# Layer 1's way back on VectorE in blocks of 32, the residual added in rows by GpSimd, the importance as a row through DRAM

## The chip, the cores and the metric

The kernel runs on one core of a Trainium2 chip. A core has TensorE (PE, matrix products and transposes), VectorE (DVE), ScalarE (ACT), GpSimd (POOL) and SyncE (SP, which here only issues transfers), 16 DMA engines, and two on-chip memories: SBUF, and PSUM, which PE writes. The metric is the device time of one execution in microseconds; lower is better. Everything is fp32.

## The reference

x has 8 images of C = 512 channels and N = 1024 positions (32 x 32). Two layers follow each other.

Layer 0: group norm (32 groups), then attention with 8 heads of 64 over all 1024 positions, a projection, and the residual: `x = x + proj(attention(norm(x)))`.

Layer 1 works on the result:

```
importance = nan_to_num(sum(xf * xf, axis=1))        # per position
idx = top_k(importance, 256)
q, k, v = wq xf, wk xf, wv xf                        # v for all positions
q_sel, k_sel = layer_norm(q[idx]), layer_norm(k[idx])
attended = softmax(clip(q_sel k_sel^T * C**-0.5)) v[idx]
out = v with its columns idx replaced by attended
x = x + wo out
```

## The kernel before, in words

Layer 0 takes 64 units (8 images, 4 pairs of heads, 2 halves of the positions). A unit has 8 blocks of scores; a list written out by hand, `SLOT`, gives the order of all steps of all units, some ahead of their unit. Beside the attention, PE fills in the projections of other images. `project_out` (line 789) makes a [128, 512] piece of the layer's output in a PSUM bank; VectorE adds bias and residual (line 796), and SP stores the piece to `x1_dram` (line 799). The bank of these fillings is a single one, so the next filling waits until it has been read.

Layer 1 (lines 244 to 605) takes one image (batch) after another. `BATCH` is one period of its order, written out by hand: each word is a step; `+` and `-` say for which batch, relative to the period, the step is done. So steps of four batches are mixed in a period. `END` is the order of the last part. All five engines keep this order, and each engine runs its instructions in order. A batch's steps, with their lines:

- `load_x1` (204) loads the image from `x1_dram`, [channel, position]. Odd batches use the tiles of layer 0's q and k, even ones a tile `x1`.
- `row` (245) transposes 128 positions on PE into a PSUM bank, four transposes of 128x128. `square` (250) sums the squares on ACT, `keep` (255) copies the rows to SBUF, `put` (258) stores them to `x_dram` from ACT's queue.
- `finite` (261) cleans the importance, a column per 128 positions. `spread` (269) makes a row of it on all 128 partitions by transposing the broadcast column on PE, 8 transposes; `imp` (277) copies it to SBUF.
- `count` (281), 8 per batch on VectorE, finds for each position how many are more important: the ones before it in order with "at least", the ones after with "more than", and within its own 128 columns the ties by a triangular mask `before`. `place`, `pick`, `holder`, `who` (328 to 357) turn the counts into the positions of the 256 chosen; `holder` is a product of PE.
- `vo` (306) gives wo wv x as rows, four products per 128 positions (wo and wv are multiplied once, at the end of layer 0); `vkeep` (314) copies them to a tile V, `vput` (325) stores them to `v_dram`.
- `getx`, `getv` (359) gather the chosen rows of x and of the values by indirect DMAs on GpSimd's queue; `vsel` (372) computes the last batch's chosen values instead.
- `selt`, `selk`, `qk` (386 to 408) make q and k of the chosen; `stats`, `root`, `norm` (410 to 437) are the layer norm, its row on VectorE, its square root on ACT; `normt`, `scale` (439 to 464) turn it back and apply weight and bias, q on ACT, k on VectorE.
- `score`, `clip`, `exp`, `probt`, `probk`, `att`, `attk` (466 to 525) are the attention of the chosen, `attput` (527) stores its 256 rows, and `fetch` (533) overwrites, by 8 indirect DMAs, the chosen rows of V.
- The way back: `back` (546) transposes V to [channel, position] on PE, four transposes for a [128, 512] piece, 8 pieces a batch; `add` (555) adds the residual on VectorE, reading the PSUM bank, and SP stores the result. `residual` (541) loads that residual from `x1_dram`, for the last two batches it is the x tile itself.

Between the layers, `begin_layer1` (1135) and `finish` (1157) do batch 0's rows, importance, counts and values beside the last projections of layer 0; `finish` puts each `count` of batch 0 between two projections.

Of the kernel before, what the change touches and what calls it, by code (L numbers as in the profile page):

```python
# [9 lines left out]
F32 = mybir.dt.float32  # L10
# [8 lines left out]
P = 128  # L19
# [20 lines left out]
BLOCKS = 2 * HALF // BLOCK  # L40
ET = mybir.EngineType
# [19 lines left out]
vkeep6- square1 inv-- put4 put2 holder- add3--- keep1 square2 back4--- att0-- att1-- who-  # L61
row6 put1 row0 add4--- row7 keep0 back7--- square0 row3 keep6 attk0-- put0 square3 vo0 row5
vput7- square6 getx- vput4- attk1-- keep3 square7 square5 add7--- vput5- back6--- keep7
finite vo1 attput-- add6--- vput0- vkeep0 keep5 selt1- selt0- spread1 spread0 fetch1-- imp1 imp0
count2 fetch0-- put6 count5 vo3 count7 vkeep1 selk1- selk0- qk1- count6 count3 qk0-
fetch5-- qk2- vput6- vput3- stats0- stats1- vput2- qk3- root0- stats2- root2- fetch2-- norm0-
vkeep3 put5 norm2- vput1- root1- vo4 vkeep4 stats3- fetch3-- norm1- vo2 root3- back0--
fetch6-- fetch4-- norm3- fetch7-- normt1- normt0- count4 vkeep2 add0-- put3 put7 back5--
normt2- normt3- scale2- scale3- row4+ add5-- back1-- scale1- count0 back2-- vo5 scale0-
count1 square4+ keep4+ place score0- score1- clip- back3-- vo6 vkeep5 pick0 add1-- exp- vo7  # L70
getv- add2-- pick1 row2+ probt- vkeep7 row1+ probk- keep2+
"""
END = """
vput2-- put4- vkeep6-- row3- add3---- square2- holder-- att1--- back4---- row0- who-- inv---
put2- row7- square1- keep1- attk1--- att0--- getx-- square3- keep3- keep0- keep7- put1- put3-
put7- row5- back6---- attk0--- row6- square7- back7---- square6- add4---- square0- square5-
keep5- keep6- put0- vput5-- vo1- put5- selt1-- finite- vkeep1- spread1- add6---- add7----
selk1-- selt0-- spread0- imp1- imp0- attput--- count1- vo0- row6 row2 vput7-- selk0-- count6-
keep6 keep2 row1 square2 count0- count2- vput6-- count7- row0 count3- vkeep0- square1 keep1
put1 vput1-- qk0-- row7 qk1-- put6- square0 put2 stats1-- qk3-- stats0-- count5- put6 keep7  # L80
square6 vo7- put7 root1-- vput1- fetch5--- row4 root0-- norm0-- qk2-- keep0 stats3--
fetch3--- count4- vo6- place- square4 vkeep7- keep4 norm1-- square7 root3-- stats2-- row3
vput0- vkeep6- vo4- normt1-- root2-- norm3-- normt0-- vput0-- row5 keep3 fetch1--- vput4--
vput3-- norm2-- vkeep4- scale1-- normt2-- put3 normt3-- scale0-- fetch2--- pick1- scale2--
square5 square3 keep5 put5 vo2- fetch0--- pick0- holder- finite spread0 scale3-- put4 vkeep2-
imp0 getv-- fetch6--- spread1 who- imp1 score0-- back2--- count4 score1-- fetch7--- count2
clip-- exp-- count3 vput2- back0--- count7 getx- vput4- count6 put0 add0--- vo3- count0
fetch4--- probt-- vkeep3- probk-- inv-- add2--- att0-- att1-- attk1-- attk0-- selt1- selt0-
selk1- selk0- attput-- count5 fetch6-- count1 qk3- place stats3- pick0 back3--- back4---
vput6- add4--- root3- pick1 back1--- qk2- fetch4-- qk0- fetch0-- norm3- add3--- fetch2--  # L90
vput7- back7--- stats2- stats0- holder fetch3-- fetch1-- qk1- who vput3- add7--- root0-
root2- add1--- back5--- norm2- getx add5--- back6--- vo5- normt3- stats1- norm0- fetch7--
root1- fetch5-- norm1- normt2- vkeep5- add6--- normt0- normt1- back2-- scale0- scale3-
scale2- back5-- back7-- vput5- add2-- back1-- add1-- selt1 back6-- back3-- scale1- add7--
add5-- score0- add6-- back0-- selt0 score1- selk1 add3-- clip- selk0 qk2 exp- stats2 back4--
qk1 probt- probk- stats1 getv- add0-- qk0 qk3 att1- root2 root1 norm2 norm1 stats0 inv-
stats3 add4-- root0 attk1- vo1 att0- root3 norm3 vkeep1 norm0 attk0- normt3 normt2 normt0
attput- scale3 normt1 fetch5- scale0 scale1 fetch7- fetch6- vo0 vkeep0 scale2 score1 fetch1-
score0 clip vsel1 fetch4- vo3 exp vselk1 vsel0 vselk0 probt fetch0- probk fetch2- vkeep3 vo6
att1 inv fetch3- att0 vo7 vkeep6 vo2 back0- attk1 back2- back4- attk0 vkeep7 back3- attput  # L100
vkeep2 add3- add0- back5- vo4 fetch7 fetch3 vo5 vkeep4 add2- back1- back7- fetch2 back6-
fetch0 fetch1 add4- add1- fetch6 add7- add5- back2 back4 add4 add6- back0 back6 fetch4 vkeep5
add0 fetch5 back3 back7 add2 back1 add6 back5 add3 add7 add1 add5
# [15 lines left out]
def attention_then_topk_attention(  # L119
# [49 lines left out]

    xp = ctx.enter_context(tc.tile_pool(name="xp", bufs=1))  # L170
# [6 lines left out]
    a_dram = [dram.tile([TOP, C], F32, tag=f"sa{b}", name=f"sa{b}") for b in range(B)]  # L177


    before = const.tile([P, P], F32, tag="before", name="before")  # L180
    iota_f = const.tile([P, TOP], F32, tag="iota_f", name="iota_f")
    token = const.tile([P, NB, 2], BF16, tag="token", name="token")

    def constants():
        w["ln_w"] = vector_of(ln_w, CT, "lw")
        w["ln_b"] = vector_of(ln_b, CT, "lb")
        make_lower_triangular(nc, before, val=1.0, diag=False)
        nc.gpsimd.iota(
            iota_f, pattern=[[1, TOP]], base=0, channel_multiplier=0,
            allow_small_or_imprecise_dtypes=True,  # L190
        )

        part = const.tile([P, 2, NB], F32, tag="part", name="part")
        nc.gpsimd.iota(
            part[:, 0, :], pattern=[[0, NB]], base=0, channel_multiplier=1,
            allow_small_or_imprecise_dtypes=True,
        )
        nc.gpsimd.iota(
            part[:, 1, :], pattern=[[P, NB]], base=0, channel_multiplier=0,
            allow_small_or_imprecise_dtypes=True,  # L200
        )
        nc.vector.tensor_copy(token, part.rearrange("p k a -> p a k"))

    def load_x1(b):

        if b % 2 and b < B - 1:
            x1[b] = [qk_tile(tag, i, f"x1_{b}_{tag}{i}") for tag in "qk" for i in range(2)]
        else:
            if b == B - 1:
                t = pools["x2"].tile([P, CT, N], F32, tag="x2", name=f"x1_{b}")  # L210
            else:
                t = xp.tile([P, CT, N], F32, tag="x1", name=f"x1_{b}")
            x1[b] = [t[:, c, :] for c in range(CT)]
        for c in range(CT):
            nc.sync.dma_start(x1[b][c], x1_dram[b][:, c, :])

    def load_layer1():
# [4 lines left out]
        load_x1(0)  # L222
# [26 lines left out]

    def square(b, j):  # L250
        norm = get("r1", ("norm", b), [P, NB], "norm", 2)
        sq = keep_pool.tile([P, C], F32, tag="sq", name=f"sq_{b}_{j}", bufs=1)
        nc.scalar.activation(sq, tiles["pt", b, j], AF.Square, accum_out=norm[:, j : j + 1])

    def keep_row(b, j):
        nc.scalar.copy(get("r1", ("xT", b, j), [P, C], "xT", XT), tiles["pt", b, j])

    def put(b, j):
        nc.scalar.dma_start(x_dram[b][ts(j, P), :], tiles["xT", b, j])
# [9 lines left out]
    def spread_row(b, j):  # L269
        pi = bank(("pi", b, j))  # L270
        for i in range(NB // 2):
            nb = j * (NB // 2) + i
            nc.tensor.transpose(
                pi[:, ts(i, P)], tiles["col", b][:, nb : nb + 1].broadcast_to([P, P]), ident
            )

    def imp(b, j):
        t = get("rp", ("imp", b), [P, N], "imp", 1)
        nc.scalar.copy(t[:, ts(j, HALF)], tiles["pi", b, j])

    def count(b, j):
# [3 lines left out]
        mine = tiles["col", b][:, j : j + 1]  # L285
        lo, hi = j * P, (j + 1) * P
        junk = tiles.get("junk")
        if junk is None:
            junk = pools["rp"].tile([P, N], F32, tag="junk", name=f"junk_{b}_{j}", bufs=1)
        if lo:  # L290
            nc.vector.tensor_scalar(
                junk[:, :lo], imps[:, :lo], mine, None, ALU.is_ge, ALU.add,
                accum_out=cnt[:, 0, j : j + 1],
            )
        else:
            nc.vector.memset(cnt[:, 0, 0:1], 0.0)
        nc.vector.tensor_scalar(  # L297
            junk[:, lo:], imps[:, lo:], mine, None, ALU.is_gt, ALU.add,
            accum_out=cnt[:, 1, j : j + 1],
        )  # L300
        nc.vector.scalar_tensor_tensor(
            junk[:, lo:hi], imps[:, lo:hi], mine, before, ALU.is_equal, ALU.mult,
            accum_out=cnt[:, 2, j : j + 1],
# [10 lines left out]
    def vkeep(b, j):  # L314
        if ("V", b) not in tiles:
            if b % 3:
                tiles["V", b] = pools["up"].tile([P, NB, C], F32, tag=f"V{b % 3}", name=f"V_{b}")
            else:
# [956 lines left out]
```

## Time and profile before

| | us |
|---|---|
| median of 3 runs | 2460.2 |
| the runs | 2457.78, 2460.20, 2460.57 |
| the profiled execution | 2458.73 |
| its span, first to last instruction | 2457.0 |

The granted clock of TensorE was 0.999 of full speed. Each group of the profile gives the line, engine and operation, what is written and read, the shapes, the number of instructions, their busy time, the mean duration of one, and the idle time of the engine just before with what ended it. PE's records are shown two to a program's fp32 product. Transfers, with the median time from issue to landing:

```profile
x<-x1d SPq DMA_DIRECT2D x20, 512.0 KB, 6.7
sa<-att SPq DMA_DIRECT2D x8, 512.0 KB, 5.4
out_dram<-x SPq DMA_DIRECT2D x16, 256.0 KB, 3.4
V<-sa,at POOLq DMA_INDIRECT x64, 3.0
```

### The profile page before, as it was taken

Reading aid. Unit: us, or ns where it says so; the run is one execution under the profiler, and the core shown is the slowest. Engines: PE = TensorE matmul, PEld = TensorE weight load, DVE = VectorE, ACT = ScalarE, POOL = GpSimd, SP = SyncE. Lnnn points to the kernel's source line nnn. Section 1 sums busy time; section 2 is a strip of 40 time slices with the busy share of each in tenths; the row PEclk is TensorE's granted clock in tenths of the full one; section 3 lists DMA queues with packets and bytes.
Section 4 is the critical chain, followed back from the end, with each engine's and each line's share of the span. In section 5 each row is a group of like instructions: output and inputs, shape, how many; then the busy total and the mean of one; then the engine's idle time right before and its main releaser. Section 6 shows DMA issues by size and latency. Waiting matters only on the chain. (4 is left out here: it accounts for less than half of the span.)

```text
span 2457.0 us, 32002 instructions
## 1 busy us (share of the span) xinstructions
PE 2410.3 (98%) x11724; PEld 967.2 (39%) x11724; DVE 1949.5 (79%) x2946; ACT 1405.2 (57%) x1828; POOL 1162.9 (47%) x557
## 2 busy tenths in 40 slices
PE   7999999999999999999999999999999999999998
PEld 3333333333333333333333333333333345555554
DVE  4899988988898889888988897889777466666683
ACT  2667666665666567656766676567656524333421
POOL 0556645655555556645655555556545501111122
PEclk9999999999999999999999999999999999999999
DMA  3011112111211120112011211112112444666553
GB/s 137 25 33 65 35 54 66 55 44 48 86 40 48 51 84 31 44 61 78 27 49 60 74 39 49 61 37 67 57 57 99 145 139 155 210 209 240 192 190 107
DMA packets 108252, 205.55 MB, mean 84 GB/s; under 512 B 19114, under 2 KB 19370, under 8 KB 108096
## 3 DMA queue, kind: packets, MB, share of 16 engines
q1 hardware_dynamic: 82432, 159.95, 19.5%
q10 hardware_dynamic: 18144, 31.48, 3.4%
q0 software_dynamic: 7520, 12.09, 1.7%
q8 instruction: 92, 1.51, 0.3%
q14 instruction: 64, 0.52, 0.1%
HBM read 146.29 MB, written 69.73 MB: 88 GB/s over the span
## 5 line engine op out<-in xcount | busy, mean ns | idle before, releaser
L1014 POOL TENSOR_TENSOR es<-es,e 128x1024 f32<-128x1024 f32 x384 | 913.6, 2379 | 61.3 <-ACT e L1009 33.2
L955 ACT COPY e<-sc 128x1024 f32<-128x1024 f32 x512 | 510.2, 1009 | 379.0 <-DVE high L961 265.9
L1006 DVE TENSOR_TENSOR e<-e,ns 128x1024 f32<-128x1024 f32 x512 | 593.7, 1210 | 0.6 <-ACT ns L1002 0.3
L1009 ACT ACTIVATE e<-e 128x1024 f32<-128x1024 f32 x512 | 532.1, 1056 | 49.6 <-DVE e L1006 36.2
L1014 POOL TENSOR_TENSOR es<-e,e 128x1024 f32<-128x1024 f32 x64 | 152.5, 2383 | 817.3 <-ACT e L1009 817.3
L947 PE MATMUL sc<-q,k 64*128 64x512 f32 x2048 | 509.9, 615 | 6.8 <-ACT e L955 6.5
L961 DVE TENSOR_TENSOR high<-sc,high 128x1024 f32<-128x1024 f32 x384 | 467.4, 1217 | 46.8 <-PE sc L947 28.3
L1022 PE MATMUL av<-e,v 128*64 128x512 f32 x2048 | 476.2, 596 | 4.6 <-DVE o L1064 3.2
L744 PE MATMUL g<-x,wqkv 128*64 128x512 f32 x1984 | 453.1, 598 | 0.7 <-ACT v L783 0.7
L947 PEld LDWEIGHTS sc<-q,k 64*128 64x128 f32 x2048 | 175.4, 185 | 309.3 <-issue 213.9
L1022 PEld LDWEIGHTS av<-e,v 128*64 128x64 f32 x2048 | 144.2, 137 | 303.8 <-issue 285.4
L744 PEld LDWEIGHTS g<-x,wqkv 128*64 128x64 f32 x1984 | 131.3, 136 | 306.9 <-issue 292.1
L744 PE MATMUL g<-wqkv,x 128*64 128x256 f32 x1920 | 220.4, 382 | 0.0
L744 PE MATMUL g<-o,wp 128*64 128x512 f32 x912 | 207.0, 595 | 0.0
L1051 DVE RECIPROCAL rs<-rs 128x256 f32<-128x256 f32 x64 | 112.1, 1751 | 94.3 <-ACT rs L1045 94.3
L744 PEld LDWEIGHTS g<-wqkv,x 128*64 128x64 f32 x1920 | 132.5, 137 | 106.0 <-issue 34.7
L534 POOL DMA_INDIRECT V<-sa,at x64 | 64.3, 1005 | 154.8 <-ACT selT L396 49.7
L961 DVE TENSOR_TENSOR high<-sc,e 128x1024 f32<-128x1024 f32 x64 | 77.6, 1213 | 59.8 <-ACT e L955 59.1
L744 PEld LDWEIGHTS g<-o,wp 128*64 128x64 f32 x912 | 64.4, 137 | 134.1 <-issue 117.9
L309 PE MATMUL b_pv<-w,x 128*128 128x512 f32 x256 | 114.1, 592 | 0.0
L405 PE MATMUL b_pp<-w,selT 128*128 128x512 f32 x256 | 112.6, 594 | 0.9 <-ACT selT L396 0.7
L363 POOL DMA_INDIRECT sel<-sx,who x16 | 16.1, 1007 | 193.4 <-PE b_po L550 47.9
(177 smaller groups left out, 1988.2 us busy)
## 6 DMA issues: line engine op xcount, KB each, us to landing
nb<-negd SPq DMA_DIRECT2D x128, 256.0 KB, 3.5
x<-in_x_dram SPq DMA_DIRECT2D x32, 512.0 KB, 5.3
ri<-rsd SPq DMA_DIRECT2D x128, 128.0 KB, 2.8
sx<-xT ACTq DMA_DIRECT2D x64, 256.0 KB, 3.3
xr<-in_x_dram SPq DMA_DIRECT2D x58, 256.0 KB, 3.4
x1d<-xr SPq DMA_DIRECT2D x58, 256.0 KB, 4.0
sv<-V ACTq DMA_DIRECT2D x56, 256.0 KB, 3.1
y<-x1d SPq DMA_DIRECT2D x48, 256.0 KB, 4.5
```

Of the source, the lines that this page charges most:

```text
L309: nc.tensor.matmul(pv, x1[b][k][:, ts(j, P)], w["vo"][:, k, :], start=(k == 0), stop=(k == CT - 1),)
L405: nc.tensor.matmul(pp, tiles["selT", b][:, k, ts(rb, P)], w["qk"[which]][:, k, :], start=(k == 0), stop=(k == CT - 1),)
L534: nc.gpsimd.indirect_dma_start(tiles["V", b][:, j, :], None, a_dram[b][:, :], bass.IndirectOffsetOnAxis(ap=tiles["at", b][:, j : j + 1], a ...
L744: nc.tensor.matmul(out[r, :], wide_[:, r], moving, start=(k == 0), stop=(k == CT - 1),)
L947: nc.tensor.matmul(sc[:, hh, :], ks[p][r, ts(j, P)], qs[p][r, ts(hf, HALF)], start=True, stop=True,)
L955: nc.scalar.copy(raw[t, j], banks["s", t, j])
L961: nc.vector.tensor_tensor(high[t], banks["s", t, j], raw[t, 0] if j == 1 else high[t], ALU.max)
L1006: nc.vector.tensor_tensor(raw[t, j], raw[t, j], high[t], ALU.add)
L1009: nc.scalar.activation(raw[t, j], raw[t, j], AF.Exp, scale=QK_SCALE)
L1014: nc.gpsimd.tensor_add(sums[t], raw[t, 0] if j == 1 else sums[t], raw[t, j])
L1022: nc.tensor.matmul(avs[t][HD * hh : HD * hh + HD, :], vs[p // 2][:, j, (p % 2) * P + HD * hh : (p % 2) * P + HD * hh + HD], e[:, hh, :], s ...
L1051: nc.vector.reciprocal(rs[:, : HALF // 2], rs[:, : HALF // 2])
```

## The change

1. Positions are taken in another order. `project_out` writes each half (512 positions) of layer 0's output to `x1_dram` with columns permuted: position 4p + j goes to column 128j + p (4 = J). VectorE reads the bank and the residual with a step of four elements and writes a new tile. A tile of 128 columns so holds the positions 4p + j of a half, and its rows in DRAM lie J apart. `put` becomes two stores of half an image on SP, 8 KB per partition.
2. The rows of x stay in a tile R, which takes the place of V as the batch's store; `vkeep` now fills one of four small tiles, `vput` stores it, and `resid` adds it to R on GpSimd. `attk` adds the chosen rows of x to the attention's result. `fetch` overwrites rows of R.
3. The way back: `back` takes 256 channels of 512 positions with four block transposes of VectorE (32x32 within [128, 256]), written with a step of four elements; `store` writes the result with four transfers of 32 partitions, in runs of 128 positions. No residual is loaded and no `add` remains. For the last batch PE does the way back as before (`pback`), copied by VectorE and ACT (`ykeep`) into one of the four tiles shared with `back`, and stored (`yput`).
4. Importance: `nput` stores the column to DRAM, `nget` loads it as a row on all partitions; `spread` and `imp` go. `count` compares with the position's half instead of its 128 columns; ties are tested over 512 columns by a mask of 516.
5. `stats`, `var`, `root`, `factor` take two blocks of rows at a time; `norm` and both halves of `scale` are on ACT. `holder` has three columns.
6. `BATCH` and `END` are new orders; periods begin at -2 and x tiles are loaded in the list's order, one of four parts a step.

The diff, cut to its core:

```
 def keep_row(b, j):
-    nc.scalar.copy(get("r1", ("xT", b, j), [P, C], "xT", XT), tiles["pt", b, j])
-def put(b, j):
-    nc.scalar.dma_start(x_dram[b][ts(j, P), :], tiles["xT", b, j])
+    nc.scalar.copy(rows(b)[:, j, :], tiles["pt", b, j])
+def put(b, h):
+    nc.sync.dma_start(
+        x_dram[b][ts(h, HALF), :].rearrange("(p j) c -> p j c", j=J), rows(b)[:, ts(h, J), :])
...
-def spread_row(b, j):
-    pi = bank(("pi", b, j))
...
+def nput(b, _):
+    nc.sync.dma_start(n_dram[b].rearrange("(h p j) -> p h j", h=NH, j=J),
+        tiles["col", b].rearrange("p (h j) -> p h j", h=NH))
+def nget(b, _):
+    nc.sync.dma_start(get("rp", ("imp", b), [P, N], "imp", 1),
+        n_dram[b].unsqueeze(0).to_broadcast([P, N]))
...
-        junk[:, lo:hi], imps[:, lo:hi], mine, before, ALU.is_equal, ALU.mult,
+        junk[:, own], imps[:, own], mine, before[:, J - j : J - j + HALF],
+        ALU.is_equal, ALU.mult, accum_out=cnt[:, 2, i : i + 1],
...
+def residual(b, j):
+    r = rows(b)[:, j, :]
+    nc.gpsimd.tensor_add(r, r, tiles["V", b, j])
...
 def normal(b, i):
-    nc.vector.tensor_scalar(
+    nc.scalar.activation(r[:, rb, :], tiles["pp", b, i], AF.Identity,
...
 def attk(b, rb):
-    nc.vector.tensor_scalar_mul(
+    nc.vector.scalar_tensor_tensor(
         t[:, rb, :], tiles["pa", b, rb], tiles["den", b][:, rb : rb + 1],
+        tiles["sel", b][:, rb, :], ALU.mult, ALU.add,
...
-def add(b, i):
-    ct, hf = divmod(i, NH)
-    y = tiles["y", b, i] if b < B - 2 else x1[b][ct][:, ts(hf, HALF)]
-    nc.vector.tensor_add(y, tiles["po", b, i], y)
-    nc.sync.dma_start(out[b, ts(ct, P), ts(hf, HALF)], y)
 def back(b, i):
+    h, g = divmod(i, 2)
+    t = pools["tp"].tile([P, N], F32, tag="T", name=f"Y_{b}_{i}")
+    for j in range(J):
+        nc.vector.transpose(
+            t.rearrange("p (s k j) -> p j s k", k=BLOCK, j=J)[:, j],
+            rows(b)[:, h * J + j, ts(g, C // 2)].rearrange("p (s q) -> p s q", q=BLOCK))
+def store(b, i):
+    t = tiles["Y", b, i].rearrange("p (s n) -> p s n", n=P)
+    d = out[b, ts(g, C // 2), ts(h, HALF)].rearrange("(s q) n -> q s n", q=BLOCK)
+    for a in range(Q):
+        nc.sync.dma_start(d[:, :, ts(a, P)], t[ts(a, BLOCK)])
...
 # project_out, empty
+    t = keep_pool.tile([P, C], F32, tag="sq", name=f"xo_{b}_{mt}_{hf}", bufs=1)
     nc.vector.scalar_tensor_tensor(
-        xr, po, pb[:, mt : mt + 1], xr, ALU.add, ALU.add,
+        t.rearrange("c (j p) -> c j p", j=J), po.rearrange("c (p j) -> c j p", j=J),
+        pb[:, mt : mt + 1], xr.rearrange("c (p j) -> c j p", j=J), ALU.add, ALU.add,
     )
-    nc.sync.dma_start(x1_dram[b][:, mt, ts(hf, HALF)], xr)
+    nc.sync.dma_start(x1_dram[b][:, mt, ts(hf, HALF)], t)
...
 # begin_layer1
     finite(0, 0)
+    nput(0, 0)
     tiles["imp", 0] = spare("imp_0")
-    also(importance(0))
-    also(importance(1))
+    nget(0, 0)
...
```

## The prediction, made before the result was known

> **What bounds the kernel now.** I read the page's busy row and its slices first, to see which engine is full and where the two layers part; then the stretches of layer 1; then the groups of the instructions that the change touches; last the order of time at both ends of layer 1. The busy row and the slices (40 of 61.4 us each):
>
> ```profile
> PE 2410.3 (98%) x11724; PEld 967.2 (39%) x11724; DVE 1949.5 (79%) x2946; ACT 1405.2 (57%) x1828; POOL 1162.9 (47%) x557
> ...
> PE   7999999999999999999999999999999999999998
> ...
> DVE  4899988988898889888988897889777466666683
> ...
> DMA  3011112111211120112011211112112444666553
> ```
>
> TensorE is full in both layers. Layer 1 begins near slice 32 (1990 us): there DVE falls to 6 tenths, DMA rises to 6. Stretches of layer 1 (us, then busy us of PE, PEld, DVE, ACT, POOL with their counts, granted clock, DMA share, GB/s):
>
> ```profile
> 1950.00:2000.00 50.00, 47.10 (x223) 21.16 (x220) 23.82 (x73) 17.25 (x44) 4.16 (x4) 1.00 0.59 200
> 2000.00:2050.00 50.00, 50.00 (x187) 27.51 (x186) 33.12 (x108) 17.57 (x40) 2.00 (x2) 1.00 0.24 84
> 2100.00:2150.00 50.00, 49.93 (x203) 27.63 (x202) 30.51 (x96) 19.59 (x45) 12.08 (x12) 1.00 0.70 244
> 2300.00:2350.00 50.00, 48.42 (x192) 26.96 (x191) 41.78 (x140) 22.36 (x50) 11.97 (x12) 1.00 0.45 154
> 2350.00:2400.00 50.00, 47.96 (x198) 27.59 (x197) 39.16 (x120) 9.34 (x22) 12.13 (x12) 1.00 0.60 197
> 2400.00:2450.00 50.00, 48.55 (x181) 27.38 (x180) 15.67 (x28) 10.45 (x20) 15.98 (x16) 1.00 0.26 87
> ```
>
> From 2000 to 2450 PE stands still for 6.3 us in all (1.0 of it between 2200 and 2250), with every other engine at two thirds or less. So an instruction taken from PE here is worth its issue time, unless a chain of waits takes its place.
>
> **What PE loses.** The end of the trace gives the price of a transpose (start us, busy us, then the group):
>
> ```profile
> 2435.13 2.35 PE L550 MATMUL b_po<-ident,V 128*128 128x128 f32 x20
> 2437.31 7.03 PE L309 MATMUL b_pv<-w,x 128*128 128x512 f32 x16
> 2444.18 3.33 PE L550 MATMUL b_po<-ident,V 128*128 128x128 f32 x29
> 2448.95 1.86 PE L550 MATMUL b_po<-ident,V 128*128 128x128 f32 x15 [1.45 <-DMA V<-sa,at]
> ```
>
> 20 transposes from 2435.13 to 2437.31 are 0.109 us each (their 273 ns are latency, pipelined); a [128,512] product of 8 records is 3.44 us. The way back has 32 transposes a batch; the last batch keeps them. 7 x 32 x 0.109 = 24.4 us. The importance's spreading has 8 a batch, in all 8 batches: 64 x 0.109 = 7.0 us. Together **-31.4 us**; a period of layer 1 shrinks from 60.5 to about 56 us of PE. The third column in `holder` I count at nothing.
>
> **What the others gain and lose, per batch.** The rows are
>
> ```profile
> L558 DVE TENSOR_TENSOR y<-b_po,y 128x512 f32<-128x512 f32 x48 | 32.1, 683 | 9.1 <-PE b_po L550 4.5 <-DMA y<-x1d 3.6 <-issue 0.6
> ...
> L434 DVE TENSOR_SCALAR rows<-b_pp,mv,nt 128x512 f32<-128x512 f32 x32 | 25.9, 809 | 1.2
> ...
> L972 DVE STREAM_TRANSPOSE mT<-high x128: 700/707/714, 58.6 to 1918.6; 128x512 f32<-128x512 f32 x128
> ...
> L987 DVE TENSOR_REDUCE neg<-four x64: 357/366/371, 62.3 to 1920.9; 32x32 f32<-32x128 f32 x64
> ```
>
> (the last two with minimum, median and maximum in ns). DVE loses 8 adds x 0.68, 4 norms x 0.81, 4 scales x 0.54 and 10 small operations x 0.16: 12.4 us. It gains 16 transposes of [128,256]; 707 ns for 512 columns and 200 for 32 put one at 0.44: 7.0 us; and counts whose tie test spans 512 columns instead of 128: 8 x (0.75 - 0.35) less three accumulator reads, +2.3. Net -3 us: 37 us of 60 become 34 of 56. ACT gets 4 norms and 4 scales (+4.6) and loses 2 copies of importance: 22 to 25. POOL gets 8 additions of half a 2.38 us row, 9.5 us, beside 12 gathers at 1.3: 25 of 56. None comes near PE. `put`, 8 issues on ACT, becomes 2 on SP; SP has 0.35 us per issue and some 33 issues a batch.
>
> [...] The only strided row here, L987 with a step of 128 bytes, shows 366 ns for 128 elements, against 352 for 128 contiguous ones (L301): nothing. I take the row for SBUF. For PSUM with a step no row is near, so both ends: 0 and doubling (+0.55 us start to start). Doubled transposes would make DVE 40 of 56, still covered. Doubled additions matter in layer 0: PE waits for that bank. Around 604 us the first addition of a slot ended 0.8 us before PE wanted the bank (604.1, 604.9), the second 0.5 (612.5, 613.0); in the next slot it was 1.0 and 1.6. One slot in four would lose about 0.7: 0 to +5, I take **+1**.
>
> The transfers: per batch 2 MB of residual are not read any more. Output goes out in 512-byte runs, 4096 packets instead of 1024. A packet of about 2 KB takes 93 ns of a DMA engine by the queue table (19.5% of 16 engines for 82432); one of 512 bytes then takes between 23 and 93: 6 to 24 us of 16 engines' time a batch, against 12 us that go (6 for the residual, 6 for the old output). DMA share 0.6 becomes 0.5 to 0.85; no wait of PE was on these.
>
> **The beginning of layer 1.** Before, importance goes over PE: `spread` at 1964.1, first count at 1966.55, all counts done at 1989.35:
>
> ```profile
> 1988.69 0.75 DVE L796 SCALAR_TENSOR_TENSOR xr_last<-last,pb,xr_last 128x512 f32<-128x512 f32 x1
> 1989.35 0.16 DVE L331 TENSOR_TENSOR place<-count 128x8 f32<-128x8 f32 x1
> ```
>
> Now the column goes out (like the 4 KB `negd`, 1.3 us) and comes back broadcast, 512 KB, between 3.5 us (the 256 KB `nb`) and 6: DVE's first count stands behind two transfers, and behind it on DVE stand the last unit's division and the last additions of layer 0. From the last `den`, d, importance is there at d+12, the counts (8 x 2.25 us) with five additions end at d+40, the picks follow. PE has finished layer 0 at d+32 and batch 1's six rows by d+36, and waits until d+41: 5 us, another 1 on the last addition. Then `who`, gather, landing (4.3 us here before) to d+49.4, where PE has only 4.3 us of rows and values to do: 2 more, and 1 for ACT's copy. 10.2 us of idle with small ones, against 2.6 before: **+7.6**.
>
> **The end.** Where the last batch's way back waits, the order has little left to give PE. From its last attention, T: `attk` T+0.9, `attput` lands T+3.9; value row 6 runs on PE to T+3.4, and GpSimd's residual for it to T+5.3, in front of 8 gathers at 1.3 us. The fourth one starts at T+10.5 and lands 3.7 later (before: 2445.23 to 2448.95). PE idles 10.8 us, then 2.6 for the last four; before the same chain (4 value rows and older way-back transposes in front) cost 1.5. Earlier waits (gather for the last batch, copies of `selT`, `sT`) 2.2. So 15.6 idle against 6.3. After PE's last transpose come `ykeep`, which waits for one of four shared buffers, and the last store: 7.2 against 6.2. **+10.3**.
>
> In between, the order leaves 11 us from `who` to the transposes of `sel` (12.5 before, with landings of 3.3 to 8.1 us), about 2 us of slack before `probt` and 4 before `holder`, counted along the order with the durations above; for a late gather here and there I put **+2** on six periods.
>
> Sum: -31.4 + 1 + 7.6 + 10.3 + 2 = -10.5. The profiled execution took 2458.7 (span 2457.0 and 1.7 around); 2448.2 by that. The median of the runs is 1.5 higher: **2449**.
>
> **Rivals.** *The waits are shorter than reckoned* (importance in 8 us instead of 12, gathers overlapping better): half of the 18 comes back, 2440. For it: in mid-layer PE idles for under 1 us per 50. Chance 0.15. *The gain is eaten, no change*: doubled additions (+4 more) and gathers landing 1 us late in six periods: 2459. 0.13. *Slower, by one mechanism: the rows of x come too late.* Layer 1 loads an x tile only when its former batch's last value row has been read, and the first transpose of its rows stands 14.6 us of PE later; before it stood over 40 later. A quarter of a tile landed 5.1 to 10.6 us after its issue, the four being issued within 3:
>
> ```profile
> DMA to landing us min/median/max: 5.1/7.4/10.6
> ```
>
> so at worst 13.6, free by 1 us. If the short packets hold the DMA engines (the 0.85 end), each us beyond 14.6 costs 6 in the layer; the result turns slower from 2.5 us over on, and at 5 over it is 2468. Against it: in that stretch no put is under way. 0.2. The main case, 2441 to 2455, has 0.52. That the PE work does not go is excluded: its instructions are gone from the program.
>
> **Numbers.** Faster by over 0.2% (below 2455.3; 0.2% is about what a measurement of this kernel can tell from no change) 0.67, within 0.13, slower 0.20. The range 2437 to 2466 leaves out some of the shortest waits and the far end of late rows; the likeliest case alone is 2441 to 2455.
>
> **What would show it.** Right: no PE group for the way back but 32 transposes, none for importance; PE idle of 5 us before `b_pn` of batch 0 and 10 us before the last `b_po`; layer 0 ending within 5 us of before; DVE transposes near 0.44 us. Wrong: PE waiting in each period for `x` or `sel` DMAs; DVE above 45 us of 56; transposes near 0.9; layer 0's end over 8 us later.

## The result, and the profile after

| | us |
|---|---|
| before, median of 4 runs | 2459.61 (2457.78 to 2460.57) |
| after, median of 4 runs | 2493.45 (2492.39 to 2494.67) |
| ratio, with its 95% interval | 1.0137 (1.0125 to 1.0149) |
| the profiled execution after, and its span | 2492.39, 2490.7 |

The change makes the kernel 33.8 us slower; I had forecast 2449, and 2466 as the upper end. PE has 288 records less, as it should (11724 before; a transpose is one record, and 7 x 32 + 64 are gone), and yet the span grew. From the page of the changed kernel:

```profile
PE 2397.8 (96%) x11436; PEld 944.7 (38%) x11436; DVE 1983.2 (80%) x2830; ACT 1434.2 (58%) x1864; POOL 1254.0 (50%) x622
```

PE's share of the span, 98% before, is 96%. Layer 0 ends where it did: the products of its last `den` on PE start at 1956.23, before at 1957.38. So the loss lies in the last 530 us. Stretches of 50 us (PE, PEld, DVE, ACT, POOL, then PE's granted clock, DMA share, GB/s):

```profile
2050.00:2100.00 50.00, 49.74 (x184) 27.10 (x183) 33.91 (x90) 19.13 (x39) 19.52 (x16) 1.00 0.47 156
2100.00:2150.00 50.00, 43.46 (x120) 20.70 (x119) 27.88 (x72) 20.83 (x44) 18.25 (x16) 0.93 0.61 187
```

Before, PE was busy for 48 to 50 of each 50 us here. From 2100 us on it stands still for 6.5 of 50, and its clock falls to 0.93, and no other engine is near its limit; the two stretches that follow have 43.2 and 42.4. So a chain of waits sets the pace. PE's waits from 1960 us on (us in all, times, longest):

```profile
PE b_ppt L510 <- ACT s L498: 23.0, 5, 4.6
PE b_po L571 <- DMA R<-sa,at: 11.1, 4, 7.2
PE b_pt L237 <- ACT R L259: 9.6, 5, 1.9
PE b_pn L351 <- DVE pick L343: 4.3, 1, 4.3
```

The second and the fourth row are the end and the beginning of layer 1, as predicted (13.4 and 5). The first and the third are new (before, PE's largest single wait from 1960 us on was 1.5 us): five times, once in each of five periods, PE waits 1.9 us for ACT to copy rows of x into a tile R, and then 4.6 us for `exp`. One such period in the order of time (start, busy us, then the group; in brackets the idle time before it and what ended it):

```profile
2101.36 5.69 DVE L554 STREAM_TRANSPOSE Y<-R 128x256 f32<-128x256 f32 x12
...
2107.08 0.58 ACT L259 COPY R<-b_pt 128x512 f32<-128x512 f32 x1 [12.44 <-DVE Y L554]
...
2107.72 0.44 PE L237 MATMUL b_pt<-ident,x_q 128*128 128x128 f32 x2 [1.93 <-ACT R L259]
...
2112.82 0.51 ACT L498 ACTIVATE s<-s,nm 128x256 f32<-128x256 f32 x1
...
2113.47 1.40 PE L510 MATMUL b_ppt<-ident,s 128*128 128x128 f32 x4 [4.60 <-ACT s L498]
```

Read it from the top. DVE's way back of a batch reads its tile R until 2107.05. ACT's first copy of another batch's rows starts 0.03 us later, after 12.44 us of idle time: there are three tiles R (`b % 3` in `rows`), so batch b + 2 gets the tile of batch b - 1, and its first copy waits until the last of the way back's four pieces has read it. Among ACT's waits from 1960 us on this is the largest (columns as for PE):

```profile
ACT R L259 <- DVE Y L554: 62.2, 5, 12.4
```

Behind this copy on ACT stand seven more copies and squares, a table load and then `exp`, whose input DVE had ready at 2101.45. PE first lacks PSUM banks, which the copies free, and then the probabilities. Batches 3 to 7 reuse a tile: five times. There is a second loss: the four transposes of the last line and the first four records of the values' product behind them (half of a [128,512] piece) take 1.19 and 3.13 us from start to start, where the same took 0.43 and 1.72 in the period before, at a clock of 1.00 (2046 to 2055). From `holder` to `holder` it is 64.7, 65.8 and 64.3 us in three successive periods. The period just before them, in which no tile R is reused yet and DVE does only one piece of a way back, takes 55.1 us (2042.72 to 2097.86).

### The profile page after: what moved, and what is told of

Its sections match the earlier page's. It is cut to its first block, busy times and chain, and to the rows that moved or that the text cites. A ratio compares the mean times of both kernels' runs of the same rounds, so it can differ in the third digit from the quotient of the medians.

```text
span 2490.7 us, 31378 instructions
## 1 busy us (share of the span) xinstructions
PE 2397.8 (96%) x11436; PEld 944.7 (38%) x11436; DVE 1983.2 (80%) x2830; ACT 1434.2 (58%) x1864; POOL 1254.0 (50%) x622
## 5 line engine op out<-in xcount | busy, mean ns | idle before, releaser
L1026 ACT ACTIVATE e<-e 128x1024 f32<-128x1024 f32 x512 | 532.0, 1056 | 50.1 <-DVE e L1023 36.3
L329 POOL TENSOR_TENSOR R<-R,V 128x512 f32<-128x512 f32 x64 | 83.8, 1321 | 123.4 <-ACT V L322 109.5
L542 POOL DMA_INDIRECT R<-sa,at x64 | 70.1, 1095 | 113.0 <-DMA sa<-att 86.5
L754 PEld LDWEIGHTS g<-o,wp 128*64 128x64 f32 x912 | 64.3, 137 | 134.8 <-issue 106.0
L416 DVE BATCH_NORM_STATS2 lbs<-b_pp 128x6 f32<-128x512 f32 x32 | 22.0, 688 | 89.1 <-PE b_pp L408 89.1
```

Source lines behind the costliest of these rows:

```text
L329: nc.gpsimd.tensor_add(r, r, tiles["V", b, j])
L754: nc.tensor.matmul(out[r, :], wide_[:, r], moving, start=(k == 0), stop=(k == CT - 1),)
L1026: nc.scalar.activation(raw[t, j], raw[t, j], AF.Exp, scale=QK_SCALE)
```

## The experiments

Theory A: the three tiles R are the root; all else follows from ACT's waiting copy and from what is queued behind it. The rivals: DVE's transposes or GpSimd's additions are slow in themselves (B, C, E), or other chains are as long as the period anyway (D). The kernel before, on the same chips, had medians of 2462.0 beside the first four kernels and 2459.8 to 2459.9 beside the others, so ratios are compared.

**`exp` ahead of the copies.**

```
-... back2- back0- back3- keep3++ keep0++ vput4 ... square2++ exp row7++ row4++ getv
+... back2- back0- back3- exp keep3++ keep0++ vput4 ... square2++ row7++ row4++ getv
```

> The changed kernel with one word of its order moved: ACT does a batch's `exp` before the first `keep` of the rows of x, not behind nine copies and squares. Theory A (ACT's `keep` waits until DVE's way back has read one of three tiles R, and `exp`, queued behind it, makes PE wait in `probt`, after which PE's granted clock is low for some us): the five waits of 4.6 us before `b_ppt` and most of the clock's loss after them (about 1.8 us each) go, 5 x 6.4 = 32 us: 2461, and no wait of PE on `s`. Its smaller wait on PSUM banks of rows (1.9 us a period) stays. Theory B (the period is long because DVE's transposes and GpSimd's additions are slow in themselves, whatever the order): PE waits the same time elsewhere, 2488 to 2494. Changed kernel so far: 2493.

Measured: 2501.9, ratio 1.0156 (1.0134 to 1.0177), no better than the change. The wait on `s` is gone, but in its place, PE's waits within one period:

```profile
PE b_st L392 <- DMA sel<-sx,who: 4.0, 1, 4.0
PE b_pt L236 <- ACT R L258: 2.0, 1, 2.0
```

`sel` is the gather of the chosen rows. GpSimd issues it behind the gather of values, which waits for the last store of these values, `vput4`, and ACT issues that store behind the same waiting copy: it left at 2174.71, the copy started at 2174.70. Theory A as I had put it failed by about 40 us: two things that others need were held, not one.

**Way back written side by side.**

```
-                t.rearrange("p (s k j) -> p j s k", k=BLOCK, j=J)[:, j],
+                t.rearrange("p (j s k) -> p j s k", k=BLOCK, j=J)[:, j],
```

> The changed kernel, but DVE's transposes of the way back write side by side and not with a step of 16 bytes; the output's columns then come in another order, the work is otherwise the same. The price of the stepped write: I predicted 0.44 us for a transpose of 128x256, the changed kernel shows 0.50 from start to start. Theory A: side by side 0.37, so the three steps of the way back that ACT's `keep` waits for end 1.6 us earlier, PE's wait before `b_ppt` is 3.0 us instead of 4.6, 5 x 1.6 = 8 us: 2485. Theory C (the stepped write is the cause of the loss): the wait is gone, 2460 or less. If the step costs nothing: 2493.

Measured: 2488.1, ratio 1.0098 (1.0077 to 1.0119), so 0.4% or about 9.6 us less than the change's 1.0137; expected 8. The twelve transposes behind `clip` take 4.03 us instead of 5.69. What became shorter is PE's wait for the copies (1.93 to 0.3); the wait before `b_ppt` stayed 4.6, since it runs from the first copy to `exp`, all on ACT. The step of 16 bytes makes the loss larger; it doesn't make it, so theory C falls.

**The way back ahead of `holder`, without and with `exp` ahead of the copies.** `fetch6-` and `fetch4-` go behind `fetch5-`, `store3--`, `back0-`, `back2-` and `back3-` in front of `holder+`:

```
-holder+ who+ clip square0++ store3-- back2- back0- back3- keep3++ ...
+store3-- back0- back2- back3- holder+ who+ clip square0++ keep3++ ...
```

> The changed kernel with words of its order moved: the last two `fetch` go right behind the third, in front of GpSimd's additions, and DVE's way back (`back0`, `back2`, `back3`) stands in front of `holder`, `who` and `clip` instead of behind them; `exp` stays behind ACT's copies. Theory A: ACT's copies can start about 4.4 us earlier relative to `holder`, so PE's wait on PSUM banks of rows (1.9 us) goes, and that before `b_ppt` falls from 4.6 to 2.7 or less, with a smaller loss of clock: 2470 to 2483. Theory B (slow in themselves): `who` and `clip` come 6 us later, and PE waits longer for the gathered rows: 2500 and more.

> Both of the former: `exp` in front of ACT's copies, and the way back in front of `holder`. Theory A: nearly all waits in the middle of layer 1 go, 5 x 8.6 = 43 us: 2450, less than the kernel before (2459.6) and about what I predicted for the change. Theory B: above 2485.

Measured: 2475.8 (ratio 1.0049, 1.0032 to 1.0065) and 2479.5 (1.0062, 1.0041 to 1.0084), a miss by 30 us. The first number is as expected, but with other waits, so it is in part luck: I had left up to 2.7 us before `b_ppt`, and none is left there. In both kernels PE now waits once a period for a bank before the values' product behind `holder`, in the first for ACT's copy, in the second for `who`, which reads the bank (one line of each):

```profile
PE b_pv L315 <- ACT R L258: 19.6, 5, 4.0
PE b_pv L315 <- DVE who L358: 17.1, 6, 3.4
```

The copy and `who` begin only when the six us of transposes on DVE are over. The wait for the way back was moved, and only in part taken away.

**A fourth tile.** The order untouched; `clip`'s mask moves into the counts' scratch tile to make room (those lines are left out below; this move was not run by itself).

```
-            if b % 3:
-                tiles["R", b] = pools["up"].tile([P, NB, C], F32, tag=f"R{b % 3}", ...
+            if b % 4:
+                tiles["R", b] = pools["up"].tile([P, NB, C], F32, tag=f"R{b % 4}", ...
```

> The changed kernel with a fourth tile R for the rows, its order of instructions untouched (the room comes from a small mask of `clip`, which now lies in the scratch tile of the counts). ACT's `keep` of a batch's rows then waits for a way back that ended a period ago. Theory A (the wait of ACT for the tile is the root, and PE's stops before rows and `b_ppt`, `sel` and the clock's loss follow from it): PE's period becomes its work, 56 to 57 us instead of 64.7, five times 8 = 40 us less than the changed kernel: 2450 to 2456, under the kernel before. Theory D (the chains of DVE, ACT and GpSimd are as long as the period without that wait, and it only shows there): the stops move to other waits as they did in the three reorderings, 2475 to 2490.

Measured: 2446.1, ratio 0.9947 (0.9930 to 0.9963): 47 us under the change and faster than the kernel before. One of the stretches of 50 us, and PE's two largest waits from 1960 us on:

```profile
2100.00:2150.00 50.00, 50.00 (x168) 24.82 (x166) 36.65 (x97) 20.71 (x43) 21.21 (x19) 1.00 0.66 209
```

```profile
PE b_po L573 <- DMA R<-sa,at: 10.9, 4, 7.1
PE b_pn L351 <- DVE pick L343: 4.3, 1, 4.3
```

PE is full, its clock is 1.00, and only the ends' waits remain; ACT no longer waits for the way back. The four periods from `holder` to `holder` take 55.14 to 55.15 us, as long as the changed kernel's period without reuse, now with the whole way back on DVE. The order, the transposes' length and GpSimd's work are those of the change, so theories B and D fall: the wait for the tile held the period.

**`vput4` and `exp` ahead of the copies, three tiles.**

```
+... vput4 square0++ ... exp keep3++ keep0++ ...
```

> The changed kernel with two words moved ahead of ACT's copies into R: `vput4` (the last store of a batch's values, which GpSimd's `getv` and behind it `getx` wait for) and `exp`. With `exp` alone PE waited for `sel` instead of `s`. Theory A': all that others need is now ahead of the waiting copy, so only PE's wait on the banks of rows (1.9 us) and some of the clock's loss stay: 59 us a period instead of 64.7, 2462 to 2470. Theory D (some other chain is as long): 2485 or more.

Measured: 2465.6, ratio 1.0026 (1.0018 to 1.0035), as expected; 58.9 to 59.6 us a period, of which PE waits 2.0 for the banks that the copies free:

```profile
PE b_pt L236 <- ACT R L258: 9.7, 5, 2.0
```

This mends the first experiment's failure: with both taken from behind the copy, the stop before `b_ppt` and the one before `b_st` are gone together.

**No additions on GpSimd.**

```
-        nc.gpsimd.tensor_add(r, r, tiles["V", b, j])
```

> The changed kernel without GpSimd's additions of the values to the rows (its output lacks that sum). Tells what GpSimd's work costs DVE. Theory A: the copies still wait for the same transposes, 2480 to 2493, though DVE's tie test falls from a mean of 956 ns to near 800 and `pick` from 491 to near 400. Theory E (GpSimd's additions hold up DVE and the fetches, and so the way back): the waits go, 2450 to 2465.

Measured: 2494.8, ratio 1.0144 (1.0127 to 1.0160). The tie test fell from a mean of 941 to 756 ns and `pick` from 491 to 347, 21 us of DVE in all, and nothing was gained:

```profile
PE b_ppt L509 <- ACT s L497: 21.8, 5, 4.6
```

Theory E falls.

**Products that keep PE busy in the wait.**

```
+        for i in range(5):
+            nc.tensor.matmul(
+                bank(("ppt", b)), ident, w["vo"][:, i % CT, :], start=True, stop=True,
+            )
```

> The changed kernel with five products of 128x128 by 128x512 put in front of the transposes of `probt` on PE, into the bank that these overwrite (work that is thrown away). They fall in PE's wait of 4.6 us. If the wait itself lowers the granted clock and that costs about 1.8 us after each: five periods save 9 us, 2484. If the clock's fall has another cause or costs nothing: 2493 or more.

Measured: 2506.1, ratio 1.0190 (1.0173 to 1.0207). In the three of eight batches without a wait the products cost 4.3 us each: 2493.5 + 12.9 is 2506.4, so the five others gained nothing. The products fill the wait before `b_ppt` (4.56 us in one period). What follows there, in the order of time:

```profile
2185.56 3.60 PE L316 MATMUL b_pv<-w,x 128*128 128x512 f32 x8
...
2190.43 0.98 PE L393 MATMUL b_st<-ident,sel 128*128 128x128 f32 x7 [1.16 <-DMA sel<-sx,who]
```

The clock is kept (1.00 from 2170 to 2195): the eight records of the values' product take 3.43 us from start to start (2185.56 to 2188.99), 0.43 each, which is full speed. But PE then waits 1.16 us for `sel`, which the same copy holds back. Counted from `holder`, PE reaches `pa` after 22.2 us here and after 22.5 in the changed kernel. So the lower clock is seen in the trace and costs nearly nothing here: without the slow stretch PE waits for `sel` instead.

**One piece of the way back earlier, three tiles.** As the kernel with `vput4` and `exp` ahead, and:

```
-... back1- score0 ... holder+ who+ clip ... back2- back0- back3- ...
+... back1- back0- score0 ... holder+ who+ clip ... back2- back3- ...
```

> Three tiles R as in the changed kernel, its order mended by three words: `vput4` and `exp` ahead of ACT's copies into R, and one of the way back's three late pieces, `back0`, moved in front of `holder`, where DVE stands idle for 1.4 us anyway. ACT's first copy can then start 2 us earlier. Theory A': PE's last large wait, that on the banks of rows (1.9 us a period), goes, while `who` comes 0.6 us later and holds PE for about as long: 57 us a period instead of 58.9, 2453 to 2459. If DVE's chain through `who` to the gathered rows is as short of time as the copies are: 2463 or more.

Measured: 2457.4, ratio 0.9989 (0.9982 to 0.9995), as expected; 57.3 to 58.3 us a period. Three words moved bring the change from 34 us over the kernel before to 2 under it, without another tile. The fourth tile is better by about 11 us: with it no copy waits for the way back, and a period takes 55.1 us; here PE still waits, in one period, 0.5 us for `who` and 0.4 for a bank that `square` reads.

## Why the prediction was wrong

The sum failed in one term: "In between, the order leaves 11 us from `who` to the transposes of `sel` ..., about 2 us of slack before `probt` and 4 before `holder`, counted along the order with the durations above; for a late gather here and there I put **+2** on six periods." I followed what each step needs from the steps that make its data, and not what its output tile needs from those that last read it. In the list, `keep3++` stands right behind `back3-`, on another engine; that `keep` writes the tile that `back3` reads is written nowhere in the order, only in `b % 3`. The term should have been +47, not +2: the change took 47.3 us more than the same order with four tiles; five periods reuse a tile, and the three measured ones take 64.3 to 65.8 us instead of 55.1. That DVE's work lies in idle time was true of the engine, and not of the tile that this work keeps.

- **PE's loss, -31.4: right.** I wrote a period of about 56 us; with the fourth tile it is 55.1 of full PE.
- **The whole sum without that term: right in the number, by some luck.** -31.4 + 1 + 7.6 + 10.3 gives 2446.2 by the profiled execution of before; the profiled execution with four tiles took 2445.98. The waits at the end were shorter than I had put them, and the clock, which I put at nothing, made up for part of it. PE's last transposes with four tiles:

```profile
2435.91 3.89 PE L573 MATMUL b_po<-ident,R 128*128 128x128 f32 x17 [1.04 <-DMA R<-sa,at]
```

  They take twice the 17 x 0.109 = 1.85 us of a full clock; the mean clock from 2400 to 2450 is 0.83. `holder` of batch 0, behind the wait of 4.3 us, takes 2.24 us, the next ones 0.55; in the changed kernel it takes the same 2.24 us, at a clock of 0.50 (1996 to 2000).
- **The beginning, +7.6: nearly.** PE waits 4.3 us before `b_pn` (I said 5), and 1.2 and 1.7 for the last addition and around `sel` (I said 1 and 3). Importance came 14.8 us after `den`, not 12, but the counts ended 39.4 us after it (I said 40).
- **The end, +10.3: the waits were a little too much.** 11.1 us before the last way back instead of 13.4, and 4.5 after PE's last transpose instead of 7.2.
- **Layer 0, +1: nothing clear.** The stepped addition is longer, 1137 ns instead of 739, but layer 0's last `den` came 1.15 us earlier in the changed kernel and 0.8 later with four tiles. That a step doubles the time, my upper end, no run shows: the addition took 0.40 us more, where I had put 0.55, and the transposes below 618 ns against 405.
- **A transpose of the way back at 0.44: too low.** In the changed kernel, and written side by side:

```profile
L554 DVE STREAM_TRANSPOSE Y<-R 128x256 f32<-128x256 f32 x112 | 54.0, 618 | 0.0
L554 DVE STREAM_TRANSPOSE Y<-R 128x256 f32<-128x256 f32 x112 | 38.1, 405 | 0.1
```

  618 ns, and 5.69 / 12 = 0.47 from start to start; side by side 405 and 4.03 / 12 = 0.34. From the row that reads with a step (366 ns against 352) I had taken that a step costs nothing in SBUF; these writes cost 213 ns more with it. By itself this cost nothing; through the tile it cost the 9.6 us of the second experiment.
- **DVE's load, 34 of 56: too low.** It is busy 36.3 of 50 us in the kernel with four tiles, 40 of 55. The transposes account for about half a us of the six (16 x 0.03), GpSimd's additions for under three (21 us in eight batches, by the run without them); the rest is open.
- **The rival "slower" named another place.** PE never waits for the load of an x tile (from 1990 us on, the parts of the tile `x` landed 5.8 to 10.3 us after their issue), so the short packets of the output did not slow PE. The right direction stood in that rival for a reason that did not happen.
- **Two slips that changed nothing.** With 2460.2 - 10.5 the sum gives 2449.7, not 2449. And "every other engine at two thirds or less" does not fit its own lines: DVE has 41.8 of 50 us from 2300 to 2350.

## What to carry to other kernels

When a result stays in place where it was made, its tile lives longer, and every order written by hand then holds waits that no word of it shows: for each tile, ask which write comes next in it, on which engine, and what stands behind that write in the queue. A wait for a tile costs by what is queued behind it. Taking away the one stop that the profile shows can bring up the next thing held by the same instruction: here `exp` alone gained nothing, `exp` and `vput4` together 27 us, another tile 47. Slack that was counted from the makers of data alone is an upper bound.

## What the runs showed of the hardware

- **The clock was at 0.50 after two short stops.** In the changed kernel, after PE's 1.9 us and 4.6 us of waiting with the transposes of two rows in between, a stretch of 2 us (columns as above):

```profile
2114.00:2116.00 2.00, 2.00 (x5) 1.33 (x6) 0.41 (x3) 1.97 (x6) 0.90 (x1) 0.50 0.73 182
```

  The mean clock is 0.67 from 2110 to 2112, 0.50 to 2116, 0.62 to 2118 and 1.00 after. By these means full speed is back about 4 us after PE resumed at 2113.47, and the fall lies within 3.1 us of PE's last transposes before the wait (2108.87). What part the wait of 1.9 us has in it, the runs leave open: in the run that kept PE busy the clock stayed 1.00 behind a wait of 1.93 us (2176 to 2184), while in the first experiment the eight transposes behind one of 1.96 took 1.62 us from start to start, where they take 0.87 in the kernel with four tiles. The slow stretch takes 2.2 us a period more than a full clock (1.19 - 0.43 and 3.13 - 1.72). In five periods this would be 11 us of the loss. The run that kept PE busy shows that almost none of it was.
- **Some of DVE's instructions lasted longer while GpSimd added.** The tie test takes 0.75 us alone and up to 1.84 beside GpSimd's additions, `pick` 0.35 and up to 1.97. Without these additions, but with the gathers, it is at most 0.81 and 0.35. Why, the runs don't show.
